# Two graph products as bfloat16 parts under a runtime branch, a shorter fixed edge loop, and reordered attention steps in a two-layer graph and transformer kernel

## The chip, the cores and the metric

The kernel runs on one core of a Trainium2 chip. The metric is the device time of one execution in microseconds; lower is better. The time before is 1946.72 us, the median of 3 runs (1946.49 to 1950.37). The engines are TensorE (PE; PEld is its weight load), VectorE (DVE), ScalarE (ACT), GpSimd (POOL) and SyncE (SP), which issues most DMAs. Each runs its own queue in order and waits for others on semaphores.

## The reference

1024 nodes with 512 features pass through two layers. The parts that the change touches are the attention of the first layer, its mixture of experts, the edges' sums, and the graph convolution of the second layer.

```python
xn = _layernorm(x)
x = x + gnn0(xn, weight, src, dst, edge_weight) + mix0(xn)      # weighted sum over edges; 2 attention + MLP blocks
x = x + experts(_layernorm(x))                                   # 8 experts, 2 per token
xn = _layernorm(x)
x = x + gnn1(xn, src, dst, ...) + mix1(xn, W_v, W_theta)
x = x + adder(_layernorm(x))                                     # three small linear layers on decoded fields

def gnn0(x, weight, row, col, vals):
    h = x @ weight.T
    return segment_sum(vals[:, None] * h[col], row)

# mix0: random-feature attention, 8 heads of 64, 256 features each
qp = ratio * (exp(q_dash - q_diag - max_over_features) + eps)
kp = ratio * (exp(k_dash - k_diag - max_over_all) + eps)
k_sum = kp.sum(axis=2)
o = einsum(ctx, qp, 1 / einsum(qp, k_sum))

# gnn1: two layers, n = 1024 nodes, 16384 edges
deg = segment_sum(ones, dst); norm = clip(deg, 1) ** -0.5
def layer(h, h0, w1, w2, b, beta):
    agg = segment_sum((h * norm)[src], dst) * norm
    f, f0 = 0.9 * agg, 0.1 * h0
    return relu((1 - beta) * (f + f0) + beta * (f @ w1 + f0 @ w2) + b)

# mix1
kv = einsum('bnd,bne->bde', X @ W_theta.T, X @ W_v.T)
return mean(X @ W_v.T) + X @ kv / (n * sqrt(d))
```

The edges' ends are drawn at random, the destinations with a square that favours low numbers. Of the 16384 edges drawn, no pair (source, destination) occurs more than 3 times, and sorted into 64 blocks of 128 sources by 128 destinations, each block filled up to a multiple of 128 edges, they make 165 chunks of 128.

## The kernel before, in words

Node rows are tiled by 128: `NT` = 8 tiles, and 512 features are `KD` = 4 chunks of 128 rows for TensorE. Matmuls write to PSUM banks in rings of two buffers (`RINGS`, L98): `bank()` takes the rings `ps`, `pd` and `pe` in turn, `bank2()` takes `pb`. The framework orders each engine's instructions ahead of time by program order and by when it reckons that they are ready, sets the semaphores, and may move an instruction ahead of earlier ones that aren't ready; `tc.keep_in_program_order` ties an instruction behind the one traced just before it on its engine. A `tc.If` block is scheduled as one unit: every engine loads the register and branches for itself.

*Edges.* In the first MLP block, `sort_edges` sorts the edges by block. In the second, `build_blocks` (L415) runs beside the MLP: over `SCHK` = 192 chunks in groups of `GRP` = 4, `one_hots` (DVE), `weighted` (ACT: 3 scalings a chunk, the weight in three bfloat16 parts) and `blocks` (PE: 4 matmuls of 128 columns a chunk, L453 and L455; DVE adds each to the block `AC` at a register's index, L459). The generator is stepped by `between()` (L782), 60 times in the block, with `per` = 48/60 steps each.

*Attention.* `prepare(pr)` lists the steps that make a head pair's keys: projections `k`, norms `kn`, key features `f` (four steps, each one `dots`), maximum `acr`, exponentials `e`, sums `tot`, and `sp`, which spreads the key sum (L600). `attend(pr)` lists the query features `f0`, `f1` (`dots` again), the denominators `m0`, `m1`, the transposes `s0`, `s1`, the contexts `c`, `ct` and the draws. `zipped` (L112) merges `attend(pr)` with `prepare(pr + 1)` by the steps' weights. `dots` (L532) runs four float32 matmuls, two row tiles for each of two heads; head 0 uses rows 0 to 63 of the array and head 1 rows 64 to 127, and each head has a bank of its own:

```python
for b in range(2):
    for h in range(2):
        r = slice(h * DH, (h + 1) * DH)
        nc.tensor.matmul(pss[h][:, b * NBF:(b + 1) * NBF],
                         a[r, (t + b) * P:(t + b + 1) * P], pj[r, i, :],
                         start=True, stop=True)
```

*Aggregation.* At L957 the blocks of `AC` with counts go to DRAM (`c_dram`, L963), and the weighted ones are multiplied by the features (L967).

*Experts.* `work` (L1170) goes over 20 tiles of 128 rows: `hidden` (two halves of 2 x 4 matmuls), between the halves `turn_next` (transposes of the next tile's rows), and one tile behind, `outputs` (8 transposes of the inner rows `h`, copies on ACT and DVE, 8 matmuls). A `tc.If` (L1203) for more than 20 tiles follows.

*Second layer.* `CT` holds the 1024 x 1024 edge counts in float32, loaded by one DMA (L1210). `z(t)` (L1290) makes the scaled features `zs`. The first product (L1333) is, for each of 8 row tiles `u`, a sum over 8 tiles `t` of a 128-wide stationary piece of `CT` against 512 columns of `zs[t]`; the result goes with `F1` through two DVE steps into `hs`. The second (L1351) has `hs` as the stationary operand and 512 columns of `CT` as the moving one, 8 groups of 8 matmuls, and gives `fT`, which `node(t)` (L1355) multiplies by `wa2`. Between the products stand 32 matmuls of `kv` (L1342). `squares` (L1299) makes `T1` and `kv` in the tag "sq". Everything here is float32.

Of the kernel before, what the change touches and what calls it, by code (L numbers as in the profile page):

```python
# [10 lines left out]
F32 = mybir.dt.float32  # L11
# [7 lines left out]
P = 128  # L19
# [9 lines left out]
SCHK += -SCHK % 4  # L29
GRP = 4  # L30
HEADS, DH, NBF = 8, 64, 256
FF = 2048
# [18 lines left out]
def tile_kernel(  # L51
# [121 lines left out]

    blk_i = srt.tile([1, 2 * P], I32, name="blk_i")
    scat_stack = ExitStack()
    scp = scat_stack.enter_context(tc.tile_pool(name="scat", bufs=1, side="right"))
# [136 lines left out]
    def sort_edges(sp):  # L313
# [90 lines left out]
        for a in range(2):  # L404
            nc.tensor.matmul(ps[0:1, a * P:(a + 1) * P], bid[:, a:a + 1], ident, start=True, stop=True)
        nc.vector.tensor_copy(blk_i, ps[0:1, 0:2 * P])

    def scatter_edges(cs):
# [6 lines left out]
    def build_blocks(bp, AC):  # L415
# [45 lines left out]

        groups = range(0, SCHK, GRP)
        hot, wtd = {}, {}
        for n in range(len(groups) + 2):
            if n < len(groups):
                hot[n] = one_hots(groups[n])
            if 0 <= n - 1 < len(groups):
                wtd[n - 1] = weighted(groups[n - 1], hot[n - 1][0])
            if n >= 2:
                blocks(groups[n - 2], *hot.pop(n - 2), wtd.pop(n - 2))  # L470
                yield

# [4 lines left out]
    for i in range(2):  # L477
        with tc.tile_pool(name="attn", bufs=2) as ap:
# [53 lines left out]
            def dots(a, t, ring):  # L532


                pss = [bank_of(ring) for _ in range(2)]
                for b in range(2):
                    for h in range(2):
                        r = slice(h * DH, (h + 1) * DH)
                        nc.tensor.matmul(pss[h][:, b * NBF:(b + 1) * NBF],  # L539
                                         a[r, (t + b) * P:(t + b + 1) * P], pj[r, i, :],  # L540
                                         start=True, stop=True)
                return pss
# [166 lines left out]
            def prepare(pr):  # L709
                k, ksq, kn = project(pr, True)  # L710
                q, qsq, qn = project(pr, False)
                f, acr, fin, e, tot, sp = key_features(pr)


                return (k[:1] + f[:1] + k[1:] + f[1:2] + ksq + f[2:3] + kn[:1] + f[3:] + q[:1] + acr + kn[1:]
                        + fin + e[:1] + q[1:] + qsq + e[1:2] + qn[:1] + e[2:3] + tot[:1] + qn[1:] + e[3:]
                        + tot[1:] + sp)

            def attend(pr):
                f0, m0, s0 = query_features(pr, 0)  # L720
                f1, m1, s1 = query_features(pr, 1)
                c, ct = contexts(pr)
                d0, d1 = draws(pr, 0), draws(pr, 1)

                return (f0[:1] + c + m0[:1] + f0[1:] + s0[:2] + m0[1:] + ct + f1[:1] + s0[2:] + m1[:1]
                        + f1[1:] + s1[:2] + m1[1:] + d0 + s1[2:] + d1)
# [28 lines left out]
        with tc.tile_pool(name="ffn", bufs=2) as fp, ExitStack() as ctx_e:  # L755
            b2 = row_bc(R_B2 + i)
            build, clear, biases, done = iter(()), [], [], 0
            per = SCHK // GRP / (2 * FF // 128 * 2 - 4)

# [22 lines left out]
            def between():  # L782
                nonlocal done
                for t in biases[:1]:
# [7 lines left out]
                while done >= 1:  # L792
                    next(build, None)
                    done -= 1
# [82 lines left out]
    with tc.tile_pool(name="route", bufs=1) as mp:  # L877
# [239 lines left out]
        with tc.tile_pool(name="moe", bufs=2) as mp, tc.tile_pool(name="mw", bufs=6) as mw:  # L1117
# [32 lines left out]

            def outputs(j, ws, h):
                hT = mp.tile([P, 8, P], F32, name="hT")
                for f in range(2):
# [7 lines left out]
                    else:  # L1161
                        nc.vector.tensor_copy(o, pt)
                ps = bank()
                for k in range(8):
# [5 lines left out]
            def work(tiles, late=None):  # L1170
                prev, xTs = None, {tiles[0]: turned_rows(tiles[0])}

                def turn_next(j):

                    if 0 < j < tiles[-1]:
                        xTs[j + 1] = turned_rows(j + 1)

                for j in tiles:
                    ws = first if j == 0 else weights(j)
                    if j == 1:  # L1180
                        outputs(*prev)
                        xTs[1] = turned_rows(1)
                    h = hidden(xTs.pop(j), ws, lambda j=j: turn_next(j))
                    if j > 1 and prev is not None:
                        outputs(*prev)
                    prev = (j, ws, h)
                if late is not None:
                    late()
                outputs(*prev)

# [16 lines left out]
    with tc.tile_pool(name="ct", bufs=1) as ctp, ExitStack() as ctx2:  # L1207

        CT = ctp.tile([P, NT, N], F32, name="CT", tag="CT")
        nc.sync.dma_start(out=CT, in_=c_dram.rearrange("(t p) d -> p t d", p=P))  # L1210

# [18 lines left out]
        xnT = lp.tile([P, KD, N], F32, name="xnT")  # L1230
        y = lp.tile([P, NT, D], F32, name="y", tag="tok", bufs=2)


# [51 lines left out]
        nc.vector.tensor_reduce(xs_, xnT, AX.X, OP.add)  # L1285


        zs = lp.tile([P, NT, D], F32, name="zs", tag="tok", bufs=2)

        def z(t):  # L1290
# [3 lines left out]
            nc.vector.tensor_add(yt, ps, rz)  # L1294
            nc.vector.tensor_scalar(zs[:, t, :], yt, norm[:, t:t + 1], None, op0=OP.mult)

        def squares(a, b, scale):  # L1299

            o = square("sq")
            for m in range(KD):
# [4 lines left out]
            return o  # L1307

        z(0)
        mirror((1, 2))  # L1310
        z(1)
        mirror((3,))
        for t in range(2, 4):
            z(t)
        T1 = squares(G, wth, 1.0)
        for t in range(4, NT):
            z(t)
        kv = squares(T1, wv, 1.0 / (N * math.sqrt(D)))
        ps = bank()
# [8 lines left out]

        hs = lp.tile([P, NT, D], F32, name="hs", tag="tok", bufs=2)
        for u in range(NT):  # L1330
            ps = bank()
            for t in range(NT):
                nc.tensor.matmul(ps, CT[:, t, u * P:(u + 1) * P], zs[:, t, :], start=t == 0, stop=t == NT - 1)  # L1333
            ps2 = bank()
            linear(ps2, xnT, F1, u)
            yt = lp.tile([P, D], F32, name="yt", bufs=3)
            nc.vector.tensor_add(yt, ps2, r1)
            nc.vector.scalar_tensor_tensor(yt, ps, norm[:, u:u + 1], yt, op0=OP.mult, op1=OP.add)
            nc.vector.tensor_scalar(hs[:, u, :], yt, 0.0, norm[:, u:u + 1], op0=OP.max, op1=OP.mult)
        for t in range(NT):  # L1340
            ps = bank()
            linear(ps, xnT, kv, t)  # L1342
            nc.vector.tensor_add(X[:, t, :], ps, X[:, t, :])
        fTs = []
        for half in range(2):
            fT = square("fT")
            fTs.append(fT)
            for m in range(KD):
                ps = bank()
                for k in range(NT):  # L1350
                    nc.tensor.matmul(ps, hs[:, k, m * P:(m + 1) * P], CT[:, k, half * 512:(half + 1) * 512],  # L1351
                                     start=k == 0, stop=k == NT - 1)
                nc.scalar.copy(fT[:, m, :], ps)

        def node(t):  # L1355
            ps = bank()
            linear(ps, fTs[t // 4], wa2, t % 4)
            ps2 = bank()
            linear(ps2, xnT, F2, t)
            yt = lp.tile([P, D], F32, name="yt", bufs=3)  # L1360
# [267 lines left out]
```

## Time and profile before

| what | us |
|---|---|
| median of 3 runs | 1946.72 |
| the profiled execution, its own time | 1944.81 |
| the profiled execution, span from first to last instruction | 1943.1 |
| PE busy from 150 to 450 (attention, MLP) of 300 | 295.92 |
| PE busy from 500 to 750 (attention) of 250 | 243.84 |
| PE busy from 750 to 1050 (MLP with blocks) of 300 | 297.97 |
| PE busy from 1250 to 1560 (experts) of 310 | 309.47 |
| PE busy from 1600 to 1680 (products of features) of 80 | 79.30 |
| PE busy from 1680 to 1845 (graph products, `kv`) of 165 | 165.00 |

The profile is one execution; its span is 1.7 us shorter than its own time. Durations of PE instructions overlap, since the next matmul starts before the one ahead of it ends. A float32 matmul shows as two records. The mean granted clock of TensorE was 0.996.

### The profile page before, as it was taken

The page shows a single profiled execution, that of the slowest core. Times are in us where ns is not written, and L with a number is a line of the kernel's source. Part 1 is how long each engine was busy: PE and PEld are TensorE (multiplying, and loading weights), DVE is VectorE, ACT ScalarE, POOL GpSimd, SP SyncE. Part 2 cuts the span into 40 slices and gives each one's busy share as a digit, 9 for nine tenths or more (in the row PEclk, how much of TensorE's full clock was granted, in tenths as well). Part 3 has the DMA queues.
Part 4 walks back from the last instruction along what each step waited for, and adds up shares of the span by engine and source line. Part 5 has one row for each costly group of instructions (what it writes and reads, how often), then busy time and mean ns, then how long its engine had stood idle before and what let it go on. Part 6 is the DMA issues. An engine that isn't in the chain of part 4 may idle for free. (4 is left out here: it accounts for less than half of the span.)

```text
span 1943.1 us, 18620 instructions
## 1 busy us (share of the span) xinstructions
PE 1903.9 (98%) x6471; PEld 907.1 (47%) x6471; DVE 763.1 (39%) x2296; ACT 601.3 (31%) x1382; POOL 207.9 (11%) x245
## 2 busy tenths in 40 slices
PE   7999999999999999999999999999999999999998
PEld 3444445444444444555554544444444445444442
DVE  4466674300456675765654411111111142111054
ACT  3456531110246655977770111101111121000011
POOL 0000000233334300011000220000000040200000
PEclk9999999999999999999999999999999999999998
DMA  6400100110110000111104396888888751000000
GB/s 231 178 33 1 44 27 27 44 44 23 44 34 2 23 23 30 50 44 47 36 22 152 116 392 231 319 299 305 317 320 311 248 204 51 0 0 0 0 17 27
DMA packets 114961, 209.88 MB, mean 108 GB/s; under 512 B 10152, under 2 KB 22256, under 8 KB 114864
## 3 DMA queue, kind: packets, MB, share of 16 engines
q1 hardware_dynamic: 102928, 186.16, 27.3%
q0 software_dynamic: 9776, 18.89, 2.7%
q10 hardware_dynamic: 2160, 3.60, 0.6%
q8 instruction: 53, 0.87, 0.2%
q14 instruction: 44, 0.36, 0.1%
HBM read 183.33 MB, written 25.30 MB: 107 GB/s over the span
## 5 line engine op out<-in xcount | busy, mean ns | idle before, releaser
L254 PE MATMUL ps<-yT,w 128*128 128x512 f32 x432 | 198.3, 598 | 0.6 <-ACT yT L225 0.6
L442 ACT ACTIVATE ow<-os,w 128x128 bf16<-128x128 bf16 x576 | 173.2, 390 | 38.3 <-PE pb L455 35.6
L411 POOL DMA_INDIRECT rec_dram<-rec,pos_e x128 | 125.0, 976 | 279.5 <-DMA rec_dram<-rec,pos_e 202.6
L254 PEld LDWEIGHTS ps<-yT,w 128*128 128x128 f32 x432 | 78.7, 190 | 92.0 <-issue 87.1
L459 DVE TENSOR_TENSOR AC<-pb,AC 128x256 f32 x192 | 80.4, 419 | 49.7 <-PE pb L455 43.5
L248 PE MATMUL pd<-w,hT 128*128 128x512 f32 x176 | 80.4, 597 | 0.0
L254 PE MATMUL pe<-yT,w 128*128 128x512 f32 x176 | 80.1, 596 | 0.2 <-ACT yT L225 0.2
L248 PE MATMUL ps<-w,hT 128*128 128x512 f32 x168 | 77.3, 598 | 0.0
L248 PE MATMUL pe<-w,hT 128*128 128x512 f32 x168 | 76.8, 596 | 0.0
L254 PE MATMUL pd<-yT,w 128*128 128x512 f32 x160 | 72.5, 596 | 0.0
L665 DVE SCALAR_TENSOR_TENSOR junk<-qe,ksb 128x256 f32<-128x256 f32 x128 | 53.6, 419 | 25.6 <-ACT qe L653 11.5
L1148 DVE TENSOR_TENSOR h<-pe,ga 128x512 f32<-128x512 f32 x14 | 9.7, 692 | 127.6 <-PE pe L1145 127.6
L585 ACT ACTIVATE kd<-kd,kb 128x256 f32<-128x256 f32 x128 | 55.9, 524 | 9.3 <-DVE kb L577 9.3
L434 DVE TENSOR_SCALAR os<-iota,rec_s 128x128 bf16<-128x128 bf16 x192 | 51.8, 271 | 15.1 <-PE pb L455 14.7
L555 ACT COPY kd<-pd 128x512 f32<-128x512 f32 x64 | 35.8, 593 | 61.3 <-PE pd L539 47.8
L653 ACT ACTIVATE qe<-pe,qb 128x256 f32<-128x256 f32 x128 | 50.3, 480 | 14.5 <-DVE qb L649 9.9
L539 PE MATMUL pe<-pj,qT 64*128 64x256 f32 x256 | 52.1, 413 | 0.0
L1148 DVE TENSOR_TENSOR h<-ps,ga 128x512 f32<-128x512 f32 x13 | 9.0, 691 | 109.2 <-PE ps L1145 101.8
L1142 PE MATMUL pd<-w,xT 128*128 128x512 f32 x112 | 51.5, 593 | 0.3 <-DVE xT L1132 0.3
L647 DVE TENSOR_REDUCE qm<-pe 128x2 f32<-128x512 f32 x64 | 42.4, 686 | 24.0 <-PE pe L539 23.4
L681 ACT COPY qp<-pb 128x512 f32<-128x512 f32 x64 | 37.1, 597 | 46.6 <-PE pb L679 46.6
L1148 DVE TENSOR_TENSOR h<-pd,ga 128x512 f32<-128x512 f32 x13 | 9.0, 691 | 107.9 <-PE pd L1145 107.9
(505 smaller groups left out, 3214.9 us busy)
## 6 DMA issues: line engine op xcount, KB each, us to landing
w<-in_ew SPq DMA_DIRECT2D x120, 1024.0 KB, 9.0
w<-in_W SPq DMA_DIRECT2D x16, 1024.0 KB, 5.2
xs_dram<-wz SPq DMA_DIRECT2D x1, 5888.0 KB, 21.4
ys_dram<-yo POOLq DMA_DIRECT2D x20, 256.0 KB
xs<-xs_dram POOLq DMA_DIRECT2D x19, 256.0 KB
c_dram<-AC SPq DMA_DIRECT2D x8, 512.0 KB, 6.0
CT<-c_dram SPq DMA_DIRECT2D x1, 4096.0 KB
w<-in_w SPq DMA_DIRECT2D x3, 1024.0 KB, 10.3
```

Source lines behind the costliest of these rows:

```text
L248: nc.tensor.matmul(ps, xT[:, k, t * P:(t + 1) * P], w[:, k, :], start=start and k == 0, stop=stop and k == KD - 1)
L254: nc.tensor.matmul(ps, w[:, k, m * P:(m + 1) * P], xT[:, k, half * 512:(half + 1) * 512], start=k == 0, stop=k == KD - 1)
L411: tc.keep_in_program_order(nc.gpsimd.indirect_dma_start(out=rec_dram[:, :], out_offset=bass.IndirectOffsetOnAxis(ap=pos_e[:, c:c + 1], axi ...
L434: nc.vector.tensor_scalar(o[:, j, :], iota[:, 0, :], rs_[:, g + j, f:f + 1], None, op0=OP.is_equal)
L442: nc.scalar.activation(ow[:, j, b, :], os[:, j, :], AF.Copy, scale=w3[:, b, g + j:g + j + 1])
L459: nc.vector.tensor_add(o, ps[:, 256 * a:256 * a + 256], o)
L539: nc.tensor.matmul(pss[h][:, b * NBF:(b + 1) * NBF], a[r, (t + b) * P:(t + b + 1) * P], pj[r, i, :], start=True, stop=True)
L585: nc.scalar.activation(kd[:, t, 0:NBF], kd[:, t, 0:NBF], AF.Exp, bias=kb[:, t:t + 1], scale=NRM)
L647: nc.vector.tensor_reduce(qm, ps.rearrange("p (b m) -> p b m", b=2), AX.X, OP.max)
L653: nc.scalar.activation(qe[:, b, :], ps[:, b * NBF:(b + 1) * NBF], AF.Exp, bias=qb[:, b:b + 1], scale=NRM)
L665: nc.vector.scalar_tensor_tensor(junk, qe[:, b, :], KEPS, kept[pr]["ksb"][:, h], op0=OP.add, op1=OP.mult, accum_out=qd[:, b:b + 1])
L1142: nc.tensor.matmul(pa, xT[:, k, :], ws[2 * f][:, k, :], start=k == 0, stop=k == KD - 1)
```

## The change

The diff does seven things. (1) `build_blocks` runs 168 chunks always and the other 24 under a `tc.If` on the number of chunks used; `between` spreads 42 steps instead of 48. (2) The matmuls of `dots` are tied in program order. (3) `prepare` and `attend` list their steps in another order, and `sp` moves from the end of `prepare` into the next `attend`. (4) In `work`, the transposes of the inner rows (`turned_hidden`) move from `outputs` to between the halves of the next tile's `hidden`. (5) The counts are loaded in 16 pieces and split into two bfloat16 matrices, multiples of 256 and the rest, whose sum is exact; the rest is summed to find whether any multiple of 256 is there. (6) `zs` and `hs` are split into three bfloat16 parts by `parts`, and both products become sums over the three parts, inside a `tc.If` whose first branch uses the low count matrix alone and whose second uses both. (7) `node` runs its `F2` matmuls ahead of those on `fT`.

```diff
@@ dots
-                        nc.tensor.matmul(pss[h][:, b * NBF:(b + 1) * NBF],
-                                         a[r, (t + b) * P:(t + b + 1) * P], pj[r, i, :],
-                                         start=True, stop=True)
+                        tc.keep_in_program_order(nc.tensor.matmul(
+                            pss[h][:, b * NBF:(b + 1) * NBF], a[r, (t + b) * P:(t + b + 1) * P],
+                            pj[r, i, :], start=True, stop=True))
@@ prepare, attend
-                return (k[:1] + f[:1] + k[1:] + f[1:2] + ksq + f[2:3] + kn[:1] + f[3:] + q[:1] + acr + kn[1:]
+                kept[pr]["sp"] = sp
+                return (k[:1] + f[:1] + k[1:] + f[1:2] + ksq + kn[:1] + f[2:3] + q[:1] + f[3:] + kn[1:] + acr
                         + fin + e[:1] + q[1:] + qsq + e[1:2] + qn[:1] + e[2:3] + tot[:1] + qn[1:] + e[3:]
-                        + tot[1:] + sp)
+                        + tot[1:])
...
-                return (f0[:1] + c + m0[:1] + f0[1:] + s0[:2] + m0[1:] + ct + f1[:1] + s0[2:] + m1[:1]
+                return (f0[:1] + kept[pr]["sp"] + c + m0[:1] + s0[:1] + f0[1:] + s0[1:2] + m0[1:] + ct
+                        + f1[:1] + s0[2:] + m1[:1]
                         + f1[1:] + s1[:2] + m1[1:] + d0 + s1[2:] + d1)
@@ build_blocks (ALWAYS = 168)
+        yield from steps(range(0, ALWAYS, GRP))
+        used = nc.values_load(used_i[0:1, 0:1], min_val=NE // P, max_val=SCHK)
+        with tc.If(used > ALWAYS):
+            for _ in steps(range(ALWAYS, SCHK, GRP)):
+                pass
@@ work
                 def turn_next(j):
+                    if j > 1 and prev is not None:
+                        prev[2] = turned_hidden(prev[2])
                     if 0 < j < tiles[-1]:
                         xTs[j + 1] = turned_rows(j + 1)
@@ second layer
-        CT = ctp.tile([P, NT, N], F32, name="CT", tag="CT")
-        nc.sync.dma_start(out=CT, in_=c_dram.rearrange("(t p) d -> p t d", p=P))
+        CT = ctp.tile([P, 2, NT, N], BF, name="CT", tag="CT")
...
+        def counts(t):
+            for h in range(2):
+                c = slice(h * 512, (h + 1) * 512)
+                raw = lp.tile([P, D], F32, name="yt", bufs=3)
+                nc.sync.dma_start(out=raw, in_=c_dram[t * P:(t + 1) * P, c])
+                big = lp.tile([P, D], F32, name="yt", bufs=3)
+                nc.vector.tensor_scalar(big, raw, 2147483648.0, None, op0=OP.add)
+                nc.vector.tensor_scalar(CT[:, 1, t, c], big, -2147483648.0, None, op0=OP.add)
+                nc.vector.scalar_tensor_tensor(CT[:, 0, t, c], CT[:, 1, t, c], -1.0, raw,
+                                               op0=OP.mult, op1=OP.add,
+                                               accum_out=over[:, 2 * t + h:2 * t + h + 1])
+
+        def parts(o, row):
+            for b in range(3):
+                nc.scalar.copy(o[b], row)
+                if b < 2:
+                    nc.vector.tensor_sub(row, row, o[b])
...
+        po = bank_of("pb")
+        nc.tensor.matmul(po[:, 0:1], ones, ov, start=True, stop=True)
+        ov_i = lp.tile([1, 1], I32, name="ov_i")
+        nc.vector.tensor_scalar(ov_i, po[0:1, 0:1], -1.0, float(NE), op0=OP.mult, op1=OP.add)
...
+        def convolutions(cs):
+            cps = [(CT[:, c], b) for c in cs for b in range(3)]
+            for u in range(NT):
+                ps = bank()
+                for t in range(NT):
+                    for n, (c, b) in enumerate(cps):
+                        nc.tensor.matmul(ps, c[:, t, u * P:(u + 1) * P], zp[b][:, t, :],
+                                         start=t == 0 and n == 0,
+                                         stop=t == NT - 1 and n == len(cps) - 1)
...
+                nc.vector.tensor_scalar(yt, yt, 0.0, norm[:, u:u + 1], op0=OP.max, op1=OP.mult)
+                parts([hb[:, u, :] for hb in hp], yt)
...
+        many = nc.values_load(ov_i[0:1, 0:1], min_val=0, max_val=NE)
+        with tc.If(many < 1) as few:
+            convolutions((0,))
+        with few.Else():
+            convolutions((0, 1))
```

`counts(t)` is traced for all tiles after the sum over `xnT` (L1285) and ahead of `z(0)`; the matmul `po` stands after `z(3)`. `z` ends in `parts` instead of writing `zs`. `kv`, the third part of `zs` and that of `hs` lie in the weight pool. The `kv` matmuls and both products stand inside `convolutions`, and all tiles that it writes are allocated ahead of the branch.

## The prediction

> **What bounds the kernel now.** I read the page's busy table and slices first, then the timeline of each stage that the diff touches, then PE's waits.
>
> ```profile
> PE 1903.9 (98%) x6471; PEld 907.1 (47%) x6471; DVE 763.1 (39%) x2296; ACT 601.3 (31%) x1382; POOL 207.9 (11%) x245
> PE   7999999999999999999999999999999999999998
> ```
>
> PE is busy in every slice, so a microsecond of PE work removed is a microsecond of time, unless another engine then makes PE wait. Busy time is modelled, so I cost PE by distances from start to start.
>
> The two graph products (L1333, L1351) in the timeline (start, length in us, then engine, line, operation, count):
>
> ```profile
> 1680.07 7.03 PE L1333 MATMUL pd<-zs,CT 128*128 128x512 f32 x16
> 1686.94 3.60 PE L248 MATMUL pe<-wf,xnT 128*128 128x512 f32 x8
> 1690.37 7.03 PE L1333 MATMUL ps<-zs,CT 128*128 128x512 f32 x16
> ```
>
> Eight float32 matmuls leave 16 records, two each. From 1680.07 to 1690.37 are 24 records: 0.429 us a record, 0.858 us a 512-wide float32 matmul, and no gap. For the price of bfloat16 I looked at the sorting and the block building:
>
> ```profile
> 320.64 0.38 PE L375 MATMUL pb<-ind,tri_bf 128*128 128x512 bf16 x1
> 320.86 1.88 PE L248 MATMUL pe<-w,hT 128*128 128x512 f32 x4
> ...
> 902.72 0.22 PE L453 MATMUL pb<-od,os 128*128 128x128 bf16 x1
> 902.77 0.33 PE L455 MATMUL pb<-ow,od 128*128 128x128 bf16 x3
> 902.94 0.22 PE L453 MATMUL pb<-od,os 128*128 128x128 bf16 x1
> ```
>
> A 512-wide bfloat16 matmul is one record, and the next one starts 0.22 us later (0.216 over all 16 of L375). Four 128-wide ones take 0.22 us, 55 ns each, with a weight load each (its own record says 98 ns): loads lie under matmuls.
>
> In attention, the same eight records of a `dots` call appear in two forms in the timeline, and the view of PE's waits (total, times, longest) names two places:
>
> ```profile
> 159.86 1.03 PE L539 MATMUL pd<-pj,kT 64*128 64x256 f32 x8
> ...
> 164.70 1.73 PE L539 MATMUL pd<-pj,kT 64*128 64x256 f32 x8 [0.87 <-DVE km L556]
> ...
> PE ps L600 <- DVE ksum L594: 5.7, 6, 1.0
> PE pd L539 <- DVE km L556: 5.3, 6, 0.9
> ```
>
> Each matmul uses 64 rows. Where heads alternate, two run at once (four pairs, 0.96 us to the next instruction); where the scheduler put both matmuls of one head first, they run mostly singly (1.66).
>
> The conditional that is there already (L1202, L1203, skipped) shows what one costs, in the view of its line (lengths in ns, first and last start) and in the timeline:
>
> ```profile
> L1203 PEldq COMPARE_BRANCH  x1: 2350/2350/2350, 1556.6 to 1556.6; - x1
> L1203 ACTq COMPARE_BRANCH  x1: 45/45/45, 1563.0 to 1563.0; - x1
> ...
> 1563.21 1.12 PE L1216 MATMUL ps<-w 128*128 128x512 f32 x2 [0.96 <-ACTq L1203]
> ```
>
> PE's sequencer reached the branch at 1556.6, while PE still had matmuls queued until 1562.25, so its 2.35 us were hidden; ACT arrived only after the last matmul, and PE stood 0.96 us for it.
>
> **The change part by part**, against the profiled execution: span 1943.1, its own time 1944.81, which is 1.9 below the median 1946.72.
>
> *Graph products.* 2 x 64 float32 matmuls, 128 x 0.858 = 109.8 us, become 2 x 64 x 3 bfloat16 ones, 384 x 0.216 = 82.9. **-26.9.** Nothing else on PE covers them, so all of it counts. From the reference's own edges no pair occurs more than 3 times, so the branch with one count matrix runs, and the 64 blocks fill 165 chunks, so the tail beyond 168 is skipped. If a weight load lay bare each time, 384 x 0.098 = 37.6 would come back.
>
> [...]
>
> *Edge blocks.* 24 of 192 chunks go: PE spends 10.7 us (L453) and 34.5 us (L455) start to start on 192, 0.235 a chunk. **-5.6**; PE is gap-free from 770 to 1021, so it counts. The 72 scalings (0.39 us) that ACT and 48 one-hots (0.26) that DVE lose were beside PE and give nothing.
>
> *Attention.* Start to start the 64 `dots` calls took 94.1 us (keys 42.3, queries 51.8); clean ones take 0.96 to 1.06, so pairing is worth at most 94.1 - 65 = 29. The pins forbid both matmuls of one head first. Moving the third and fourth key calls apart should clean most of the keys' excess of 10 us; in the queries' 19 the two halves of a call also lie up to 3.7 us apart, since other dots became ready, and I take under half: 8 and 8. Of the waits (11.0), `sp` placed after the next dots loses perhaps half of 5.7. A pinned call now waits for its second bank (copy 0.59 and maximum 0.68 us), where before PE did the first head's other matmul: +3. Together **-16**; bounds -40 (all 29 and 11) to +53 (below).
>
> *The edges' conditional.* After the last chunk DVE must load the count and branch (0.32 + 0.08 us in the L1202/L1203 rows), PE must wait for that where it waited 1.72 us for the block additions: **+0.8**, bounds 0 to 4 (a bare 2.35 jump plus that). Queued behind it on SP is the first expert load (1022.5, needed at 1121.8), on DVE the first `xc` sum, 7 us later.
>
> *The products' conditional.* Entry: the count is known some 30 us earlier, and PE's sequencer runs ahead, so 0 to 1. Exit: PE jumps over the second branch, twice as long, beneath its queue; ACT leaves only after the last copy of `fT` began, like the 0.96 above, plus a possible jump of its own; POOL enters after its eight additions of L1326 (1681 to 1691) and waits for nobody. `node` then runs F2 first, which needs no `fT`, but not before the exit. **+2.5**, bounds 1 to 10.
>
> *Counts and parts.* The 4 MB load becomes 16 loads and 48 DVE instructions: 16 x (0.49 + 0.49 + 0.75) = 27.7 us by L1295 and L1247. `parts` adds 24 copies of 0.58 on ACT and 16 subtractions of about 0.61 on DVE before the products. The stage now, in the view of windows (PE, PEld, DVE, ACT, POOL busy; clock; DMA):
>
> ```profile
> 1600.00:1680.00 80.00, 79.30 (x230) 40.05 (x231) 17.42 (x26) 12.72 (x26) 1.29 (x1) 1.00 0.11 40
> ```
>
> DVE goes from 17.4 to about 55 of 80, ACT from 12.7 to 27: they fit. But counts stand ahead of the first `z` on DVE; if none is hoisted into DVE's gaps, they run from 1617.6 (end of the L1285 sum) to about 1648, while PE needs a bank back that `z(0)` holds at 1642: 6 us. The sum's matmul stands after `z(3)`, at 1635, and would wait as well unless passed. Behind a load that waits for its buffer on SP stand the weights of L1255 to L1257, issued at 1599 to 1601 now and used from 1635. DVE has some 20 us of gaps before 1624, so most is hoisted: **+2**, bounds 0 to 12. The last `z` ends 17 us before the products, its chain of seven steps lasts about 5. In the first product a row takes PE 8.6 us against DVE 3.1 and ACT 1.7.
>
> *Inner rows.* The 8 transposes of a tile move ahead of the next half; PE has no gap from 1160 to 1500, so 0, and up to 3 where a third transpose waits for a bank.
>
> Sum: -26.9 - 5.6 - 16 + 0.8 + 2.5 + 2 = **-43.2**; 1944.8 becomes 1901.6, and at the median 1946.7 becomes about **1903.5**.
>
> **Rivals.**
>
> A, *attention gives nothing and the conditionals lie bare* (0.20): pairing is eaten by bank waits, each of four crossings costs 2.35 + 0.47 (ACT's load), counts cost 6: -32.5 + 11.3 + 6 = -15.2, **1931**. For it: the 2350 ns row. Against: PE's queue covered it there. [...]
>
> B, *attention pays in full* (0.12): -32.5 - 40 + 5.3 = -67, **1880**. For it: clean calls of 0.96 us in each head pair; against: the banks are freed 1.3 us apart.
>
> C, *slower: the pins make PE stand* (0.08). Place: every `dots` call, whose second matmul may no longer be passed by its own head's. Price: a bank's copy and maximum, 1.28 us, 64 x 1.28 = 82, less 29 of pairing: +53; -32.5 + 5.3 + 53 = +26, **1973**. It decides from 0.88 us a call, where it has eaten both the pairing and the rest. For it: the 0.87 waits before L539 now; against: unpinned projections and transposes can fill the time.
>
> D, *weight loads lie bare* (0.02): -26.9 becomes +10.8, **1941**. The 55 ns step speaks against it.
>
> E, *the other branch is taken* (0.02): 384 more matmuls x 0.216 = +83, **1986**. The edges speak against it.
>
> **Numbers.** The forecast has 0.56: 1890 to 1918 alone. The range, 1884 to 1932, reaches to A and most of the way to B; what lies outside is C, E, D and B's far half, under 2 in 10. Faster by over 0.2% (3.9 us, about what can be told from no change): forecast, A, B, and D's better half, with a cut for trouble in the schedule I don't see: 0.88. Within: 0.03. Slower: C, E: 0.09.
>
> **What would show it.** The products: 24 bfloat16 records from row to row of 5.2 us, 384 in all at 0.216; if 0.31, D. Blocks: 672 records where 768 were. Attention: eight-record groups of L539's successor near 1.0, their sum near 78; if PE's waits at that line exceed 20 us, C. At both conditionals PE's idle under 3 us; if 5 or more, A. DVE's counts done before 1640. I am wrong altogether if PE's idle time, 39 us now, grows by more than 30.

## The result, and the profile after

The changed kernel takes 1934.66 us, the median of 10 runs (1927.14 to 1944.38); the kernel before, on the same chip, takes 1948.28 (10 runs, 1945.94 to 1951.57). The ratio is 0.9936, with a 95% interval of 0.9922 to 0.9951: faster by 0.6%, some 12 to 14 us, where 43 were forecast. 1934.66 lies 2.7 us above the upper end of the range given, 1932. The profiled execution took 1929.99 us, with a span of 1928.3 and a mean granted clock of TensorE of 0.992 (0.996 before), as a share of full speed.

First come the busy table and two rows of the slices, as they were shown of before, with the row of the granted clock added.

```profile
PE 1863.4 (97%) x6505; PEld 881.9 (46%) x6505; DVE 793.7 (41%) x2323; ACT 608.2 (32%) x1358; POOL 208.7 (11%) x245
PE   7999899999999989999999999999999999899998
...
PEclk9999999999999999999999999999999999899998
```

PE's busy time fell by 40.5 us and the span by 14.8. Where before PE was filled from the second slice to the last but one, three of those slices now fall below 9: one in each of the two attentions (the fifth and the fifteenth) and one at 1640. In the third of these the clock dips as well.

The graph products in PE's timeline of the changed kernel (start, length, line, operation, count):

```profile
1697.43 3.60 PE L250 MATMUL pe<-wf,xnT 128*128 128x512 f32 x8
1700.86 5.34 PE L1397 MATMUL ps<-zs,CT 128*128 128x512 bf16 x24
1706.04 3.60 PE L250 MATMUL pd<-wf,xnT 128*128 128x512 f32 x8
```

24 records from 1700.86 to 1706.04 are 0.216 us each. Each of the two products went from 54.9 to 41.4 us.

The two attentions, in the view of PE's waits over the whole program (total, times, longest). Before, its two large rows were 5.7 and 5.3.

```profile
PE pb L688 <- DVE qe L680: 7.9, 16, 0.6
PE pb L530 <- ACT qp L690: 7.5, 6, 1.3
PE pb L572 <- DVE rd L678: 4.7, 6, 1.1
PE pd L548 <- ACT kT L509: 3.6, 4, 0.9
PE ps L609 <- DVE ksum L603: 3.4, 2, 1.7
```

The wait for the key maximum is all but gone and the one for the key sum is smaller. New ones stand at the transposes of the queries (L688), of the norms (L530) and of the key maximum (L572). Which of them come from tying the `dots` and which from the new order of steps, the runs below tell apart.

The stage in which the counts are made, in PE's timeline of the changed kernel:

```profile
1631.79 3.60 PE L250 MATMUL pe<-Fz,xnT 128*128 128x512 f32 x8
1635.23 1.02 PE L1357 MATMUL ps<-w,G 128*128 128x512 f32 x2
1645.05 0.56 PE L1369 MATMUL pb<-ov,ones 128*128 128x1 f32 x2 [8.80 <-DVE ov L1335]
1645.47 5.47 PE L1357 MATMUL ps<-w,G 128*128 128x512 f32 x6
1650.73 3.92 PE L1357 MATMUL pd<-w,G 128*128 128x512 f32 x8
```

PE stands 8.8 us for `ov`, the sum of what overflows the first count matrix. Then six records take 5.26 us to the next start, where eight take 3.43 at the full clock.

Where the time went, by the starts of PE's matmuls in the two traces (after minus before):

| up to | shift, us | this part, us |
|---|---|---|
| last draw of the second attention (738.6, 745.4) | +6.8 | +6.8 |
| last edge block | +0.9 | -5.9 |
| last aggregation matmul (1084.7, 1086.2) | +1.5 | +0.6 |
| first matmul of the second layer's stage | +0.7 | -0.8 |
| first record of the first product (1680.1, 1692.2) | +12.2 | +11.5 |
| end of the span, with both products | -14.8 | -27.0 |

### The profile page after: what moved, and what is told of

The parts are those of the page before. It is cut to its first block, busy times and chain, and to the rows that moved or that the text cites. A ratio compares the mean times of both kernels' runs of the same rounds, so it can differ in the third digit from the quotient of the medians.

```text
span 1928.3 us, 18768 instructions
## 1 busy us (share of the span) xinstructions
PE 1863.4 (97%) x6505; PEld 881.9 (46%) x6505; DVE 793.7 (41%) x2323; ACT 608.2 (32%) x1358; POOL 208.7 (11%) x245
## 5 line engine op out<-in xcount | busy, mean ns | idle before, releaser
L445 ACT ACTIVATE ow<-os,w 128x128 bf16<-128x128 bf16 x504 | 151.8, 389 | 44.7 <-PE pb L458 41.4
L462 DVE TENSOR_TENSOR AC<-pb,AC 128x256 f32 x168 | 70.4, 419 | 55.4 <-PE pb L458 48.5
L565 DVE TENSOR_REDUCE km<-pd 128x1 f32<-128x512 f32 x64 | 41.6, 684 | 41.1 <-ACT kd L564 41.1
L437 DVE TENSOR_SCALAR os<-iota,rec_s 128x128 bf16<-128x128 bf16 x168 | 46.5, 278 | 14.4 <-PE pb L456 14.4
L1159 PE MATMUL pe<-w,xT 128*128 128x512 f32 x112 | 50.3, 592 | 0.0
L208 ACT ACTIVATE sd<-sd 128x1 f32<-128x1 f32 (+2 forms) x39 | 8.0, 204 | 133.2 <-DVE sd L207 122.8
## 6 DMA issues: line engine op xcount, KB each, us to landing
xs_dram<-wz SPq DMA_DIRECT2D x1, 5888.0 KB, 21.4
w<-in_w SPq DMA_DIRECT2D x3, 1024.0 KB, 10.6
```

Of the source, the lines that this page charges most:

```text
L445: nc.scalar.activation(ow[:, j, b, :], os[:, j, :], AF.Copy, scale=w3[:, b, g + j:g + j + 1])
L462: nc.vector.tensor_add(o, ps[:, 256 * a:256 * a + 256], o)
L1159: nc.tensor.matmul(pg, xT[:, k, :], ws[2 * f + 1][:, k, :], start=k == 0, stop=k == KD - 1)
```

## The experiments

A matmul tied by `tc.keep_in_program_order` is called pinned here. Two theories stood at the start. *Attention*: the pins pair the `dots` (pairs of records that run at once went from 156 to 248, the calls from 94.1 to 72.7 us start to start), and what that saves comes back as waits that the pins make; the rival was the moved steps. *Counts*: the 12 us are the place of one matmul, not the counts' work on DVE. Each run was timed beside the kernel before on its own chip, where that kernel's median lay between 1946.96 and 1948.51. Here are all the runs that compute the whole; three that leave work out come later. In the columns, us is the median, "dots" and "query transposes" are sums from the start of each matmul to the start of PE's next one, which counts a wait with the matmul ahead of it, and "draw" is the start of the last draw of the second attention, all three from the one profiled execution of the run.

| pins / order of steps / overflow sum | us | ratio, 95% | dots | query transposes | draw |
|---|---|---|---|---|---|
| before | 1948.28 | 1 | 94.1 | 34.0 | 738.6 |
| all / new / early (the change) | 1934.66 | 0.9936 (0.9922 to 0.9951) | 72.7 | 50.0 | 745.4 |
| none / old / early | 1926.16 | 0.9885 (0.9863 to 0.9906) | 95.8 | 34.0 | 740.9 |
| all / old / early | 1931.54 | 0.9919 (0.9900 to 0.9939) | 76.9 | 35.8 | 743.8 |
| none / new / early | 1924.10 | 0.9886 (0.9861 to 0.9910) | 85.3 | 36.5 | 737.2 |
| keys / new / early | 1926.72 | 0.9889 (0.9867 to 0.9910) | 84.9 | 36.6 | 739.2 |
| first query call / new / early | 1937.53 | 0.9942 (0.9919 to 0.9966) | 80.8 | 43.2 | 747.8 |
| all but that call / new / early | 1921.94 | 0.9865 (0.9839 to 0.9891) | 74.5 | 38.7 | 734.6 |
| all / new / late | 1922.40 | 0.9878 (0.9854 to 0.9901) | 72.7 | 49.9 | 745.4 |
| none / new / late | 1913.86 | 0.9822 (0.9803 to 0.9841) | 85.4 | 36.6 | 737.5 |
| all but that call / new / late | 1911.41 | 0.9815 (0.9792 to 0.9839) | 74.6 | 38.7 | 734.9 |

**The attention as it was, all else changed.** The pins go, and `prepare` and `attend` get their old lists of steps:

```diff
-                        tc.keep_in_program_order(nc.tensor.matmul(
-                            pss[h][:, b * NBF:(b + 1) * NBF], a[r, (t + b) * P:(t + b + 1) * P],
-                            pj[r, i, :], start=True, stop=True))
+                        nc.tensor.matmul(pss[h][:, b * NBF:(b + 1) * NBF],
+                                         a[r, (t + b) * P:(t + b + 1) * P], pj[r, i, :],
+                                         start=True, stop=True)
```

> Attention as before the change (no pins, steps in the old order), all else as changed. Theory: the pairs of the dots saved 21 us of PE, and waits for the query features, the key sums and half-clock windows in attention took back 28, so without the attention change the second attention ends some 6.8 us earlier than in the changed kernel: about 1928 median, and runs spread less than the 17 us of the changed kernel, since fewer half-clock windows fall. Rival: the attention change is worth its pairs and only the place differs, then 5 us or more slower than the changed kernel, about 1940.

1926.16 us: 8.5 less than with the new attention, and the intervals of the two ratios lie apart. So the attention's part of the change is a loss, though it pairs the calls. (The last draw starts 2.3 us later than before in the same code: this execution had 6.8 us at half clock at 590.6, which the profile of before has not.)

**The overflow sum behind z(7).** The matmul at L1369 and its conversion move past four `z` and all of `T1`:

```diff
         for t in range(2, 4):
             z(t)
-        po = bank_of("pb")
-        nc.tensor.matmul(po[:, 0:1], ones, ov, start=True, stop=True)
...
         for t in range(4, NT):
             z(t)
+        po = bank_of("pb")
+        nc.tensor.matmul(po[:, 0:1], ones, ov, start=True, stop=True)
```

> The matmul that sums the counts stands after the last z instead of after z(3), all else as changed. Theory: PE stood 8.8 us at that matmul for the last of the counts and then ran 6 us at half clock; with it behind 28 us of other matmuls both go, 10 to 12 us off, about 1923. Rival: DVE's backlog of counts holds the banks of the z anyway, then PE waits at the third group of T1 for z(0)'s bank instead, and no more than 5 us go.

1922.40 us, 12.3 less. In PE's timeline of this run, at the same place:

```profile
1635.07 3.60 PE L1357 MATMUL ps<-w,G 128*128 128x512 f32 x8
1638.51 3.60 PE L1357 MATMUL pd<-w,G 128*128 128x512 f32 x8
1643.31 3.70 PE L1357 MATMUL pe<-w,G 128*128 128x512 f32 x8 [1.21 <-DVE yt L1346]
```

Of the wait, 1.2 us is left, and eight records take 3.43 us again. The view of windows (length, PE and PEld and DVE and ACT and POOL busy, granted clock, DMA share, GB/s), first of the changed kernel and then of this run, shows the second half of the price:

```profile
1640.00:1680.00 40.00, 34.95 (x76) 15.68 (x77) 21.92 (x42) 16.39 (x29) 0.00 (x0) 0.87 0.03 7
```

```profile
1640.00:1680.00 40.00, 38.79 (x92) 17.05 (x91) 21.91 (x42) 18.15 (x32) 0.00 (x0) 1.00 0.03 8
```

The clock of 0.87 is one stretch of 10.2 us at half speed that begins at 1641.1, within the wait. Its last 6.3 us lie after PE resumed and cost half of that, 3.2; 8.8 + 3.2 less the 1.2 that is left are 10.8, and the first product's last record starts 10.8 earlier (1757.5 to 1746.7). DVE does the same work in both (21.9 us): the counts' work itself costs the end nothing beyond the 1.2.

Why DVE was late is in the view of the tile `yt` on DVE, in the changed kernel (durations in ns, first and last start; then what DVE waited for, us and times):

```profile
L1264 DVE TENSOR_SCALAR yt<-yt x16: 390/427/428, 1570.0 to 1641.9; 128x512 f32<-128x512 f32 x16
...
L1266 DVE SCALAR_TENSOR_TENSOR CT<-CT,yt x16: 655/692/694, 1597.8 to 1643.5; 128x512 bf16<-128x512 bf16 x16
...
  DMA yt<-c_dram: 24.5, 11
```

The first count began at 1570.0, but its third step, which frees the buffers, stands in DVE's order behind other work and ran at 1597.8. `yt` has three buffers for the loads and the copies alike, so the second count began at 1598.5 and the other loads followed a few at a time, each 2.8 us to landing. DVE waited for them 11 times, 13.6 us of the 24.5 ahead of the first count; the last count ended at 1644.2. Whether buffers of their own, or another place for that third step, would end it sooner wasn't tried.

**Pins alone, and order alone.**

> The steps of attention in the old order, the pins kept, all else as changed. Theory: the pins give the pairs (dots near 73 us start to start, from 94) and the new order of steps makes the new waits at the query transposes, so this is the fastest in attention: 10 us or more below the changed kernel, about 1922. Rival: the pins themselves make the waits, since pinned dots no longer let other work pass; then as slow as the changed kernel, 1935.

> The steps of attention in the new order, no pins, all else as changed. Theory (the new order makes the waits): slower than the changed kernel, by up to the 21 us of pairs that are lost, 1940 to 1955. Rival (the pins make them): faster than the changed kernel, 1922 to 1930.

With the pins alone 1931.54, with the new order alone 1924.10, with neither 1926.16. The pins cost 5.4 us in the old order, where the intervals of the ratios still touch, and 10.6 in the new one, where they lie apart; the new order alone gains about 2, inside the intervals. It pairs the keys by itself (34.9 us without a pin, 34.5 with all). So the pins make the loss, and all that they add in pairs is in the queries (50.4 to 38.2). Not every new wait is theirs: without a pin the new order also has 5.1 us at the norms' transpose (six waits of 0.85, up to 1.26 with the pins) and 4.0 at the key maximum's.

**Which pins.** Three runs, each with one of the conditions below: pins on the keys' calls only, on all calls but the first query call of each head pair (token blocks 0 and 1), and on that call alone:

```diff
-                        tc.keep_in_program_order(nc.tensor.matmul(
+                        mm = nc.tensor.matmul(
...
+                        if ring == "pd":                # keys only
+                        if ring == "pd" or t > 0:       # all but the first query call
+                        if ring == "pe" and t == 0:     # the first query call only
+                            tc.keep_in_program_order(mm)
```

> The changed kernel with the pins on the key dots alone; the query dots are free. Theory: the order alone pairs the keys (34.9 us without any pin), so pins there do nothing, and the cost of the pins sits in the query calls: 1921 to 1927, the draws of the second attention last at 736 to 739, the query transposes near 36 us. Rival: a pin on any call fixes what stands around it on PE: draws last at 743 to 746, query transposes 45 us or more, 1929 to 1935.

1926.72 us: the intervals show no loss from pins on the keys (1924.10 without). The draws start at 739.2, 0.2 beyond the bound given, with two half-clock stretches of 3.4 us at 230.8 and 237.6.

> The changed kernel with every dots call pinned but one in each pair of heads: the first query call (token blocks 0 and 1), with which a pair's attention begins, is free. Theory (the pins cost at the boundary between two pairs alone: held in the written order, the next pair's first query dots can't be put between the last transposes and draws of the pair before, so these stand bare, and each waits for the bank that ScalarE still evicts): query transposes 34 to 40 us, the wait for qp below 3 us (7.5 in the changed kernel), draws of the second attention last at 730 to 737, 1917 to 1924. Rival (each pinned query call costs a little where it stands): transposes 44 to 50, draws last at 742 to 746, 1928 to 1935.

> The opposite cut: only that first query call of each pair is pinned, the other query calls and all key calls are free. Theory (the boundary): the whole loss of the pins comes back with it, query transposes 44 to 52 us, draws of the second attention last at 742 to 747, 1929 to 1936, although only 8 of 64 dots calls are pinned. Rival: transposes 34 to 39, draws last at 736 to 739, 1921 to 1927, as with no pins.

This settles the attention. With 56 of 64 calls pinned it takes 1921.94 and the draws start at 734.6; with only the other 8 pinned it takes 1937.53, no faster than the whole change, and the draws start at 747.8. (The transposes, 43.2, stay 0.8 short of the range given, and the time and the draws lie 1.5 and 0.8 beyond theirs.) The interval of the first lies apart from that with all calls pinned, and that of the second from that with none. The timelines of PE follow where the third head pair's queries end and the fourth's begin in the second attention, first of the kernel before:

```profile
699.79 0.66 PE L679 MATMUL pb<-ident,qe 128*128 128x128 f32 x4
700.38 1.13 PE L539 MATMUL pe<-pj,qT 64*128 64x256 f32 x6
701.35 0.40 PE L521 MATMUL pb<-ident,sq 64*128 64x64 f32 x4
```

then of the changed kernel:

```profile
701.82 0.72 PE L688 MATMUL pb<-ident,qe 128*128 128x128 f32 x4 [0.52 <-DVE qe L680]
703.01 0.72 PE L688 MATMUL pb<-ident,qe 128*128 128x128 f32 x4 [0.47 <-DVE qe L680]
704.99 0.46 PE L530 MATMUL pb<-ident,sq 64*128 64x64 f32 x4 [1.26 <-ACT qp L690]
...
707.07 3.01 PE L705 MATMUL ps<-qp,cx 128*64 128x512 f32 x6 [0.17 <-ACT qp L690]
710.01 1.14 PE L548 MATMUL pe<-pj,qT 64*128 64x256 f32 x8
```

and with that one call free:

```profile
692.56 0.30 PE L690 MATMUL pb<-ident,qe 128*128 128x128 f32 x1 [0.52 <-DVE qe L682]
692.79 0.70 PE L548 MATMUL pe<-pj,qT 64*128 64x256 f32 x2
693.42 0.55 PE L690 MATMUL pb<-ident,qe 128*128 128x128 f32 x3
693.90 0.70 PE L548 MATMUL pe<-pj,qT 64*128 64x256 f32 x2
694.52 0.66 PE L690 MATMUL pb<-ident,qe 128*128 128x128 f32 x4
```

The next pair's first `dots` are PE's only ready work at this boundary. Free, they are put between the last transposes of the pair before, and cover the time in which DVE makes `qe` and ACT evicts `qp`. Pinned, they stay behind the draws (710.01), and the transposes stand one behind the other with nothing between: from 701.82 to 705.38 PE needs 3.6 us for some 1.5 us of work (0.59 for four transposes of queries and 0.33 for the norms' in the kernel before). It happens at each boundary between two pairs, six times in the program: in every profile with that call pinned, under either order, its `dots` start behind all draws of the pair before at all six boundaries, and in every one with it free they start ahead of the last seven or eight records of these draws. In the old order with all pins they stand even behind the key sum (711.04 at this boundary); there the transposes lose little (35.8), and the wait of 7.3 us, six times, is at the norms' transpose.

**What holds the rest.** With one call free the `dots` are 19.6 us shorter than in the kernel before, of which 4.0 reach the draws. Three runs leave out the denominators of the queries' features, so they don't compute the attention: the two multiplications with a sum along the row and the reciprocal go, and DVE's chain between exponential and transpose is about half.

```diff
-                        for b in range(2):
-                            junk = ap.tile([P, NBF], F32, name="junk", bufs=1)
-                            nc.vector.scalar_tensor_tensor(junk, qe[:, b, :], KEPS, kept[pr]["ksb"][:, h],
...
-                        nc.vector.reciprocal(rd, qd)
...
-                            nc.vector.tensor_scalar(qe[:, b, :], qe[:, b, :], KEPS, rd[:, b:b + 1],
+                            nc.vector.tensor_scalar(qe[:, b, :], qe[:, b, :], KEPS, 1e-4,
                                                     op0=OP.add, op1=OP.mult)
```

> The changed kernel, pins and new order as it has them, without the denominators of the queries' features: the two multiplications with a sum along the row and the reciprocal of each head and step are left out, and the scaling uses a constant, so the output is not the reference's. It shortens VectorE's chain between the exponentials and the query transposes by about a half. Theory (the pins are not wrong in themselves, they bring PE to the query transposes earlier than VectorE can have their input): the wait at the transposes (50.0 us from start to start, 7.9 of it named as a wait for qe) falls to 30 to 38, the draws of the second attention end by 727 to 735, and this kernel is at least 5 us faster than the same without pins. Rival (the pins make PE stand for what ScalarE evicts, whatever VectorE does): the draws end above 738, the waits for qp and kT stay at 7 and 3 us, and the kernel without pins is faster by 5 us or more, as it is with the whole chain.

> As the run before it, without the pins (the new order stays): the denominators are left out in the same way, so the output is not the reference's. Theory: without pins PE fills the time with other work already, so the shorter chain brings little: the draws of the second attention end at 732 to 737 (737.2 with the whole chain), query dots stay unpaired near 50 us. Rival: the chain bounds the attention with pins or without, and the draws end below 730 here as well.

Both theories fell, and both rivals held but for the sizes of the waits. With all pins 1925.46 (ratio 0.9879, 0.9857 to 0.9901), draws at 739.8; without pins 1913.52 (0.9826, 0.9803 to 0.9849), draws at 724.4. By the medians the shorter chain brings 9.2 us with the pins and 10.6 without, and the pins cost what they did (11.9 here, 10.6 with the whole chain). The draws come 5.6 and 12.8 us earlier, but the pinned profile has 20.5 us at half clock in the attention and the free one none, so they can't be compared as they stand. The waits of the pinned one:

```profile
PE pb L530 <- ACT qp L682: 14.2, 6, 2.4
PE ps L609 <- DVE ksum L603: 3.4, 2, 1.7
PE ps L522 <- ACT sq L514: 2.4, 5, 0.5
PE pb L680 <- ACT qp L682: 1.2, 6, 0.2
```

The wait for DVE's `qe` has gone, and PE waits at the next link, six times as before: the ring `pb` has two banks, and PE waits until ACT has copied one out. So what the pins run into isn't DVE's chain, but the lack of other work at the boundary.

> As the run with one query call of each pair free, and without the denominators of the queries' features (the two multiplications with a sum along the row and the reciprocal are left out, a constant in their place), so the output is not the reference's. The dots' pairs are worth 19.6 us there (94.1 to 74.5), of which 4.0 reach the end of the attention's draws (738.6 to 734.6). Theory (VectorE's chain of the queries holds the rest back: without it PE's shorter dots come through): the draws of the second attention last at 712 to 722, below the 724.4 of the same cut without pins. Rival (ScalarE's evictions and the two banks hold it, whatever VectorE does): 724 or later.

1912.94 us (0.9817, 0.9794 to 0.9839), draws at 727.6: by the numbers given this is the rival, and a wait for ACT's `qp` of 7.8 us, six times, is back at the norms' transpose. But this profile has 10.2 us at half clock before 700 and the free one above has none; half of it, 5.1 us, is more than the 3.2 between the two. So this run decides nothing: what share DVE, ACT and the banks have in the rest stays open.

**Both cures together.**

> The changed kernel with two edits: the dots are not pinned (the new order of the attention's steps stays), and the matmul that sums the counts' overflow stands behind z(7) in place of z(3). Theory: the two losses are independent, so the gains add: 1934.66 - 10.6 (order only, 1924.10) - 12.3 (sum late, 1922.40) = 1912, the draws of the second attention last near 738, 'w,G' near 15 us, ratio to the kernel before 0.980 to 0.984. Rival: a half-clock window comes with the wait or the clock falls elsewhere, so that only the larger of the two is kept: 1918 to 1924.

> As the run with one query call of each pair free, and the matmul that sums the counts' overflow stands behind z(7). Theory: the two add, 12 us under that run, 1905 to 1912, and below order only with the late sum (1913.86). Rival: what the pins pair is lost in waits of VectorE's chain, and it is 1912 to 1918, the same as without pins.

1913.86 us without pins, near the 1912 expected of two independent losses; 1911.41 with all but the first query calls pinned. The intervals of these two overlap, so the pairing of the queries isn't shown to pay in the total. Either is faster than the kernel before by 1.8% and than the change by 1.1 to 1.2%.

## Why the prediction was wrong

**Graph products: right.** -27.0 against -26.9. A step of 0.216 us with a weight load of 98 ns each (`LDWEIGHTS` of L1397 and L1416, 192 each) ends the rival in which loads lie bare: that would have made it 0.31 (0.216 + 0.098). 192 records a product show the one-matrix branch.

**Edge blocks: right.** -5.9 against -5.6; 672 records.

**The conditionals: right, and cheaper at the second.** At the edges' one PE's timeline after shows, where 1.72 us were before:

```profile
1024.76 5.42 PE L981 MATMUL pe<-hw,AC 128*128 128x512 f32 x12 [2.34 <-DVEq L478]
```

The part between the blocks and the last aggregation matmul is +0.6 against +0.8. The products' conditional, in the view of its line (ns, first and last start):

```profile
L1423 PEldq COMPARE_BRANCH  x2: 80/1866/3653, 1685.9 to 1826.2; - x2
L1423 ACTq COMPARE_BRANCH  x2: 38/39/40, 1690.0 to 1830.3; - x2
```

The jump over the other branch takes PE's sequencer 3.65 us, but it gets there at 1826.2, while PE has matmuls queued of which the last starts at 1829.85; the next one starts at 1830.06. +2.5 was forecast, no idle time is seen. The edges' wait was cheap by chance in this profile: the same 2.3 us stand in all thirteen profiles of the changed kernel and its variants, and in nine of them a stretch of 3.4 us at half clock follows, 1.7 us more by estimate (half of 3.4). Rival A's time, 1931, lies near the measured one, but by other terms: its bare crossings (+11.3) didn't come, and the attention lost where A had it at nothing.

**Attention: the step that failed.** The forecast was -16, the measured part +6.8. The pairing came, and larger than worked out: the calls sum to 72.7 us where 78 were named. "A pinned call now waits for its second bank: +3" looked inside the call, and there little happened (3.6 us at L548, for `kT`). What was missed is that a pin also ties the call's first matmul behind all that was traced ahead of it, so that the next pair's work can't be brought forward. From start to start, +16.0 at the query transposes, +9.2 at the projections, +4.0 at the key sum and +3.6 at the norms eat the 21.4 and more. Of these, 11.3 at the transposes and 3.0 at the key sum go when that one call is free, and with them the 12.7 us between 1934.66 and 1921.94. The other two aren't this call's doing alone: with it free the projections keep +8.2, of which +6.4 is there with the new order and no pins at all, and the norms keep +3.8, which is gone only without any pin on the queries (15.8 us, where the kernel before has 15.7). Rival C had pins that make PE stand, but inside each call, the wrong place, and its sign and price for the whole, +26, are far off. The two half-clock stretches of 3.4 us in the attention are in the +6.8.

**Counts: sized wrongly.** +2 was taken of 0 to 12, and +11.5 came. The text named the cause as a case ("the sum's matmul stands after z(3), at 1635, and would wait as well unless passed") and set it aside because DVE has gaps before 1624 into which most of the counts should go. DVE had the gaps, but the first count held the buffers until 1597.8 and the others' loads came after that, so the counts ended at 1644.2, where 1640 was named as the sign. The matmul wasn't passed: PE's later ones stood behind it.

**Inner rows:** 0 forecast, -0.8 for the experts.

**The terms together.** With +6.8 for -16 and +11.5 for +2 the forecast of -43.2 becomes -10.9; without the second conditional's 2.5 and with the experts' -0.8 it is -14.2, and -14.8 was measured. No term was kept for the clock. PE's idle time grew by 25.7 us (39.2 to 64.9), just under the 30 named as the sign of being wrong altogether.

## What to carry to other kernels

Here a pin for the order inside a group also fixed the group's place in the queue, and freeing one group per head pair took 12.7 us off: leave a group free that starts a new phase, and look in the timeline at what used to fill the gap ahead of it. A small matmul that only feeds a branch belongs as late in PE's queue as the branch allows: here PE stood 8.8 us at one while some 28 us of other matmuls stood behind it. Before work is called hidden on an engine with gaps, follow its loads and its buffers: here the gaps passed while one early piece of work, begun at 1570.0, held the buffers until 1597.8.

## What the runs showed of the hardware

In the changed kernel a gap on PE was paid twice: 8.8 us at the overflow sum, and behind it 6.3 us at half speed, in which six records took 5.26 us where eight take 3.43. In the clock records of these profiles half speed comes in stretches that are multiples of 3.4 us (in the changed kernel 3.41, 6.83 and 10.24), except the last, which the end of the program cuts off (5.9). Each stretch in the attention of the changed kernel (at 142.7 and 705.9) began after 3.4 us in which PE was busy 49% by its matmul records; in the runs that followed, the share ahead of a stretch in the attention was between 0.31 and 0.68 (0.68 at 590.6 in the run with the old attention). The wait for the sum came with a half-clock stretch of 6.8 to 13.7 us in all ten profiles with the early sum, and none of the three with the late one has a stretch there. Gaps aren't the whole story: a stretch of 3.4 us at 1091.6 has no gap before it (PE is busy in all of the 3.41 us ahead) and is in the kernel before too, at 1089.0. There the 3.4 us ahead of it hold, beside four transposes, matmuls of 8 columns and of 1; whether that is its cause wasn't tried.

The spread goes with the clock: the ten runs of the changed kernel go from 1927.14 us at a clock of 0.993 to 1944.38 at 0.983. Half speed all the time would read 0.5 (10.2 us of it in 40 read 0.87), so the 0.010 between them is some 39 us at half speed, 19 us of work by this estimate; 17.2 were measured. In each of the kept profiles every stretch begins on one grid of 3.413 us, and where the grid lies against the start of the program differs: 0.11 us in the kernel before, 2.73 in the changed one, from 0.04 to 3.15 in the runs. The same 2.3 us of wait at the edges' conditional has a stretch behind it in nine profiles and none in four. So the same wait cost more in some profiles than in others; that the place of the grid decides it, and makes the spread, is the author's estimate and was not shown. These are single executions of different kernels; for the ten runs of the changed kernel the place of the grid wasn't recorded.
